# A graph layer on one Trainium2 core: attributes put into PSUM ahead of the gathering matmuls, sums by node moved to other banks

## The chip, the core and the metric

The kernel runs on one core of one Trainium2 chip. The core has a matrix engine (TensorE, PE in the profile; its weight loads stand as PEld), VectorE (DVE), ScalarE (ACT), GpSimd (POOL) and an engine that only issues transfers (SP). Matmuls write PSUM, which VectorE and ScalarE read and write; it has eight banks of 512 float32 numbers per partition. The metric is the time of one execution in microseconds (us) on the device. The kernel before took 1771.63 us, the median of 3 runs (1760.12 to 1772.58).

## What is computed

A graph of 6250 nodes and 206250 edges, 64 numbers per node and per edge, everything float32. The edges are sorted by `dst`, the node at which an edge ends.

```python
h = jnp.maximum(_layernorm(x, axis=-1), 0.0)
msg = jax.nn.relu(h[src] + edge_attr)
agg = jax.ops.segment_sum(msg, dst, num_segments=x.shape[0])
t = jax.nn.relu((h + agg) @ W1 + b1)
out = x + t @ W2 + b2
```

The large part is the middle: for each edge a row of `h` is fetched, the edge's attribute is added, and the results are summed by node.

## The kernel before

**Groups and units.** The edges are cut into 269 groups of 768: 128 partitions with 6 columns, one edge per partition and column. The rows of the first five groups are fetched by GpSimd with indirect transfers. From group 5 on, half of each group's columns (3 of 6) still come that way (`xg`), and the other 3 are fetched by TensorE; in 12 groups ("whole") all 6 columns are, as two runs of 3. Such a run of 3 columns is a unit. There are 276 units, and the main loop `for u in range(U): half(u)` (line 792) runs once for each.

**Fetching on TensorE.** All of `h` lies in SBUF, split into three bfloat16 parts that add up to the float32 value (`hp`). Fetching takes two steps, and each works on one-hot matrices that VectorE and ScalarE write ahead of time (`found`, `backs`). First, `slots_of` (line 470) collects rows of `hp` with matmuls of 32 output rows into a PSUM tile `half`, two runs of 192 numbers per tile (3 parts of 64), and `slots_out` (line 485) copies that tile on ScalarE as bfloat16 to `picked`. Two units share a set of six such tiles. Then `pick` (line 488) makes 18 matmuls of 128 by 128 by 192, six for each column, that bring each edge's three parts to its partition, in a PSUM tile `pick0` or `pick1`, by the parity of the unit.

**The four places of a column.** A pick tile holds 4 columns of 4 places of 64 numbers, two banks in all. For each of 3 columns, places 0 to 2 take the three parts. `room` (line 496), a ScalarE copy, puts the edge's attribute in place 3. VectorE then adds the four places in one reduction of 768 numbers to 192 (line 563).

**Sums by node.** `messages` (line 553) adds the DMA-fetched rows to their attributes (line 560), makes the reduction (line 563), and ScalarE writes `msg`, the relu of the group (line 565). `window_sum` (line 570) multiplies the message of a unit with a one-hot matrix of 32 nodes (`one_hot`, line 540): 12 matmul records for 6 columns. Its result, 32 numbers wide, stands in the fourth column of the pick tile of that unit's parity. `sum_into_z` (line 536) adds it to `z`, the sum of all nodes, on VectorE, two units later.

**Order.** The schedule is written out by hand. Each engine runs its queue in the order in which the code issues the work, and the framework sets the waits between engines; for PSUM it does so by bank: two engines that touch a bank are kept apart, in whatever columns. In `half(u)` the order is: loads (SP); `window_sum(u - 1)` (PE); `room(u + 1)` (ACT); twice `slots_of` and `slots_out` for the next set, and a third `slots_of`; `pick(u + 1)` (PE); `sum_into_z(u - 2)` (DVE) and, for blocks of nodes that are complete, the final layers (`blocks_behind`); `messages(u)` (DVE, then ACT); the third `slots_out` (ACT); `one_hot(u)`, and the writing of later `backs` and `found` (DVE, and on ACT `back_far`, line 455, or `back_near`, line 458). Ranks for later sets follow in small pieces.

So ScalarE's queue in a half reads: room, copy, copy, message, copy, then one of the two for `backs`. VectorE's reads: add into `z`, add of `xg`, reduction, one-hot, `backs`, `found`.

**PSUM.** The eight banks are: two pick tiles of two banks, three `half` tiles that take turns, and one tile `rows` for everything else. The attribute loads go to twelve SBUF tiles `ea` that take turns.

Of the kernel before, what the change touches and what calls it, by code (L numbers as in the profile page):

```python
# [81 lines left out]
def kernel(  # L82
# [102 lines left out]
    nc.vector.memset(z[:D, N:], 0.0)  # L185

    def attr_load(ea, g):
        if g < NG:
            nc.sync.dma_start(out=ea.rearrange("p j d -> p (j d)"),
                              in_=edge_attr[g * GE:(g + 1) * GE, :].rearrange("(p j) d -> p (j d)", j=G))  # L190
        else:
            nc.sync.dma_start(out=ea[:, G - CT:G - 1].rearrange("p j d -> p (j d)"),
                              in_=edge_attr[C * P:(C + TJ) * P, :].rearrange("(p j) d -> p (j d)", j=TJ))
            nc.sync.dma_start(out=ea[:, G - 1, :], in_=edge_attr[E - P:, :])
# [16 lines left out]
    def load(g):  # L211
        ea = edge.tile([P, G, D], F32, name="ea")
        attr_load(ea, g)
        lo, hi = first_col(g), pool_cols(g)
        if is_whole(g):
            return ea, None
        if g < F0:
            xg = lnp.tile([P, G, D], F32, name="xr", bufs=F0)
        else:
            xg = edge.tile([P, G - H, D], F32, name="xg")  # L220
        gather(xg[:, lo:], src_sb[:, g * G + lo:g * G + hi], hi - lo, x if g < RAW else h_rows)
        return ea, xg
# [99 lines left out]
    def source(c):  # L322
# [12 lines left out]
        nc.sync.dma_start(out=lines[c].rearrange("k m s -> m k s"), in_=col.rearrange("m (k s) -> m k s", k=SETS))  # L335

    def ln_head(r, n):
        xv = x_rows(r, n)
# [22 lines left out]
    def ln_turn(r, m, h):  # L361
        zv = z[:D, :NP].rearrange("d (p r) -> d p r", r=RR)
        for i in range(0, m, 4):
            n = min(4, m - i)
            pt = psum.tile([D, 4, PP], F32, name="half", bufs=3)
            for u in range(n):
# [103 lines left out]
    def slots_of(k, n0):  # L470
        ps = psum.tile([P, 2, 3 * D], F32, name="half", bufs=3)
        for u in range(2):
# [15 lines left out]
    def pick(u0, cols):  # L488
        k, i = divmod(u0, 2)
        ps = picks[u0]  # L490
        for u in cols:
            for q in range(Q):
                nc.tensor.matmul(ps[:, u, :3].rearrange("p t d -> p (t d)"), backs[k][:, q, i * H + u, :],  # L493
                                 picked[k][:, i * Q + q], start=(q == 0), stop=(q == Q - 1))

    def room(u):
        g, c0 = UNITS[u]
        picks[u] = pick_banks[u % 2]
        nc.scalar.copy(picks[u][:, :H, 3], taken[g][0][:, c0:c0 + H])  # L499

# [52 lines left out]
    def messages(u):  # L553
# [7 lines left out]
        if u >= 0:  # L561
            c0 = UNITS[u][1]
            nc.vector.tensor_reduce(ea[:, c0:c0 + H], picks.pop(u)[:, :H].rearrange("p j t d -> p j d t"), AX.X, ALU.add)  # L563
        msg = work.tile([P, G, D], F32, name="msg", bufs=3)
# [180 lines left out]
    for k in (0, 1):  # L745
        source_load(k)
        spot_load(k)
    for g in range(F0):
        enter(g + AHEAD)
        messages(g - F0)  # L750
# [67 lines left out]
    with tc.If(any_left > 0):  # L818
        nc.gpsimd.iota(wide, pattern=[[1, WB]], base=1, channel_multiplier=0, allow_small_or_imprecise_dtypes=True)
        with tc.For_i(0, NG, 1) as i:  # L820
# [3 lines left out]
            nc.vector.tensor_copy(lf, left[:, ds(i * G, G)])  # L824
            ea = edge.tile([P, G, D], F32, name="ea")
            nc.sync.dma_start(out=ea.rearrange("p j d -> p (j d)"),
# [3 lines left out]
            all_windows(combine(xa, ea, G), lf, G)  # L830
        ea = edge.tile([P, G, D], F32, name="ea")
        attr_load(ea, NG)
# [45 lines left out]
```

## Time and profile before

| | before |
|---|---|
| time, median of 3 runs | 1771.63 us (1760.12 to 1772.58) |
| time of the profiled execution | 1747.93 us |
| its span, first to last instruction | 1746.2 us |
| from `window_sum` in half(0) to the last one | 115.92 to 1737.88 us, 276 halves, 5.88 us each |
| VectorE busy, ScalarE busy | 1024.7 us (59%), 871.5 us (50%) |
| mean granted TensorE clock | 0.907 |

The profiled execution ran 1.3% below the median; 1.7 us of it lie outside of the span. The page of the profile gives busy time by engine, then the chain of work that ended last, followed back from the end, then the costliest groups of instructions with mean durations in ns and the idle time before them. "Issue" stands for time in which an engine waited for nothing that the profile shows, and "remote" for a release that it can't name. Other views show the waits in total, and the timeline: start, length, engine, line, operation, what it writes and reads, how many alike, and in brackets the idle time before it and what ended it. Matmuls are pipelined, so a busy TensorE isn't one at its peak.

### The profile page before, as it was taken

The page shows a single profiled execution, that of the slowest core. Times are in us where ns is not written, and L with a number is a line of the kernel's source. Part 1 is how long each engine was busy: PE and PEld are TensorE (multiplying, and loading weights), DVE is VectorE, ACT ScalarE, POOL GpSimd, SP SyncE. Part 2 cuts the span into 40 slices and gives each one's busy share as a digit, 9 for nine tenths or more (in the row PEclk, how much of TensorE's full clock was granted, in tenths as well). Part 3 has the DMA queues.
Part 4 walks back from the last instruction along what each step waited for, and adds up shares of the span by engine and source line. Part 5 has one row for each costly group of instructions (what it writes and reads, how often), then busy time and mean ns, then how long its engine had stood idle before and what let it go on. Part 6 is the DMA issues. An engine that isn't in the chain of part 4 may idle for free.

```text
span 1746.2 us, 54838 instructions
## 1 busy us (share of the span) xinstructions
PE 1302.7 (75%) x23181; PEld 991.3 (57%) x23181; DVE 1024.7 (59%) x2686; ACT 871.5 (50%) x1955; POOL 802.7 (46%) x798
## 2 busy tenths in 40 slices
PE   3047787778778778777777877877777877777787
PEld 2035566556557556565655655655665655565566
DVE  7346556546565665555755655654566566465576
ACT  4235455446455555554544544644554555454465
POOL 6734435444453553544544444444444445444430
PEclk9998889889897898989988988987899889898898
DMA  6223334334333442443433333333333334333341
GB/s 181 66 57 108 103 93 109 91 88 114 99 98 95 114 109 82 108 106 93 117 96 91 106 99 95 104 98 90 94 103 106 93 106 110 86 103 95 97 111 33
DMA packets 115095, 172.34 MB, mean 99 GB/s; under 512 B 28443, under 2 KB 83612, under 8 KB 114844
## 3 DMA queue, kind: packets, MB, share of 16 engines
q1 hardware_dynamic: 89752, 143.03, 27.4%
q0 software_dynamic: 25088, 25.74, 8.3%
q8 instruction: 184, 3.01, 0.7%
q14 instruction: 67, 0.55, 0.1%
q10 hardware_dynamic: 4, 0.01, 0.0%
HBM read 164.85 MB, written 3.84 MB: 97 GB/s over the span
## 4 chain that ended last, share of the span: by engine, by line
PE 64%; issue 18%; another core or an unknown queue 7%; ACT 6%; DVE 3%; POOL 1%; DMA 1%; DVEq 0%; ACTq 0%; POOLq 0%
PE pick L493 28%; PE half L478 24%; PE pick L575 8%; ACT picked L486 2%; PE rows L329 1%; ACT msg L565 1%; PE rows L592 1%; PE rows L603 1%; ACT dist L455 1%; PE rows L279 1%; POOL xg L198 1%; PE rows L277 1%; PE rows L315 0%; ACT backs L458 0%
## 5 line engine op out<-in xcount | busy, mean ns | idle before, releaser
L198 POOL DMA_INDIRECT xg<-h_rows,src_sb x754 | 768.0, 1019 | 865.4 <-DVE ea L560 688.2
L478 PE MATMUL half<-hp,found 128*32 128x192 bf16 x14352 | 500.8, 260 | 215.3 <-issue 191.8
L486 ACT CAST picked<-half 128x384 bf16<-128x384 f32 x828 | 381.1, 477 | 521.7 <-remote 321.7
L493 PE MATMUL pick<-picked,backs 128*128 128x192 bf16 x4968 | 574.6, 267 | 83.9 <-issue 64.2
L493 PEld LDWEIGHTS <-backs 128*128 128x128 bf16 x4968 | 446.6, 106 | 198.1 <-issue 179.6
L478 PEld LDWEIGHTS <-found 128*32 128x32 bf16 x14352 | 340.7, 100 | 320.7 <-issue 284.0
L538 DVE TENSOR_TENSOR z<-z,pick 128x32 f32 x281 | 53.1, 189 | 656.7 <-issue 236.4
L563 DVE TENSOR_REDUCE ea<-pick 128x192 f32<-128x768 f32 x276 | 262.5, 951 | 0.0
L465 DVE TENSOR_SCALAR backs<-spots,ids 128x768 bf16<-128x768 int16 x690 | 251.0, 415 | 0.0
L575 PE MATMUL pick<-oh,msg 128*64 128x32 f32 x3224 | 177.3, 237 | 54.6 <-ACT msg L565 29.5
L446 DVE TENSOR_SCALAR found<-sources,nodes_of 128x1536 bf16<-128x1536 int16 (+1 forms) x414 | 212.4, 542 | 0.1
L575 PEld LDWEIGHTS pick<-oh,msg 128*64 128x64 f32 x3224 | 138.4, 149 | 119.7 <-issue 53.7
L565 ACT ACTIVATE msg<-ea 128x384 f32<-128x384 f32 (+2 forms) x281 | 144.4, 514 | 24.5 <-DVE ea L563 12.8
L499 ACT COPY pick<-ea 128x192 f32<-128x192 f32 x276 | 88.6, 321 | 126.0 <-remote 69.4
L458 ACT ACTIVATE backs<-dist,ones 128x768 bf16<-128x768 bf16 x138 | 130.5, 946 | 0.3 <-ACT dist L455 0.3
L455 ACT ACTIVATE dist<-spots,far 128x768 bf16<-128x768 int16 x138 | 129.9, 941 | 0.0
L544 DVE TENSOR_TENSOR oh<-slot,slots 128x192 f32<-128x192 int16 (+2 forms) x281 | 95.7, 341 | 24.2 <-remote 24.2
L560 DVE TENSOR_TENSOR ea<-ea,xg 128x192 f32<-128x192 f32 x252 | 90.2, 358 | 3.4 <-issue 1.9
L277 PE MATMUL rows<-at,upper 128*128 128x432 f16 x46 | 17.0, 369 | 44.9 <-remote 24.1
L281 ACT CAST before<-rows 128x432 f16<-128x432 f32 x46 | 23.6, 514 | 48.4 <-remote 38.8
L332 ACT CAST source<-rows 24x64 int16<-24x64 f32 x138 | 27.6, 200 | 35.9 <-remote 27.6
L329 PE MATMUL rows<-holds,marks 128*96 128x96 f16 x276 | 27.6, 235 | 15.2 <-DVE oh L544 4.9
(102 smaller groups left out, 435.1 us busy)
## 6 DMA issues: line engine op xcount, KB each, us to landing
sources<-source_row SPq DMA_DIRECT2D x138, 384.0 KB
ea<-in_edge_attr_dram SPq DMA_DIRECT2D x268, 192.0 KB
spots<-spot_rows SPq DMA_DIRECT2D x138, 192.0 KB
xg<-h_rows,src_sb POOLq DMA_INDIRECT x754
xb<-in_x_dram SPq DMA_DIRECT2D x12, 128.0 KB
out_dram<-o SPq DMA_DIRECT2D x12, 128.0 KB
h_rows<-x SPq DMA_DIRECT2D x3, 384.0 KB
dst_sb<-in_dst_main_dram SPq DMA_DIRECT2D x1, 804.0 KB
```

Of the source, the lines that this page charges most:

```text
L198: nc.gpsimd.indirect_dma_start(out=xg[:, j, :], out_offset=None, in_=rows[:, :], in_offset=bass.IndirectOffsetOnAxis(ap=idx[:, j:j + 1], a ...
L446: nc.vector.tensor_scalar(found[k][:, b * PARTS:b * PARTS + n].rearrange("p m i s -> p (m i s)"), sources[k][:, :n * 2 * S], nodes_of[:, b ...
L455: nc.scalar.activation(dists[k], spots[k].bitcast(I16), AF.Abs, bias=far)
L458: nc.scalar.activation(backs[k][:, Q - 1].rearrange("p t s -> p (t s)"), dists.pop(k), AF.Relu, bias=ones[:, 0:1], scale=-1.0)
L465: nc.vector.tensor_scalar(backs[k][:, q].rearrange("p t s -> p (t s)"), spots[k].bitcast(I16), ids[:, q:q + 1], None, op0=ALU.is_equal)
L478: nc.tensor.matmul(ps[j * S:(j + 1) * S, u], found[k][:, m, i, :], hp[:, min(m, RR - 1)].rearrange("p t d -> p (t d)"), start=(b == 0), st ...
L486: nc.scalar.copy(picked[k][:, n0:n0 + 2], halves.pop((k, n0)))
L493: nc.tensor.matmul(ps[:, u, :3].rearrange("p t d -> p (t d)"), backs[k][:, q, i * H + u, :], picked[k][:, i * Q + q], start=(q == 0), stop ...
L544: nc.vector.tensor_tensor(oh[:, lo:hi], slot[:, g * G + lo:g * G + hi].unsqueeze(2).to_broadcast([P, n, W]), slots.unsqueeze(1).to_broadca ...
L563: nc.vector.tensor_reduce(ea[:, c0:c0 + H], picks.pop(u)[:, :H].rearrange("p j t d -> p j d t"), AX.X, ALU.add)
L565: nc.scalar.activation(msg[:, lo:hi], ea[:, lo:hi], AF.Relu)
L575: nc.tensor.matmul(pa[i * D:(i + 1) * D], msg[:, j, :], oh[:, j, :], start=(j < lo + 2), stop=(j >= hi - 2))
```

## The change

The attribute no longer has a place of its own. `room` now writes all three places of each column before the matmuls: the attribute in place 0, zeros in places 1 and 2. All 18 matmuls of `pick` accumulate onto that (none starts afresh any more), and VectorE adds three places instead of four. The zeros come from the attribute tiles, which become twice as wide: 12 fixed tiles `eas` whose second halves ScalarE fills with zeros once, before the main loop (`tails_begin`). In the usual unit the attribute and the zeros lie so that one copy of 576 numbers writes them; a unit on columns 0 to 2 of a whole group takes two copies. The result of `window_sum` moves from the pick tiles to the columns 384 to 511 of the three `half` banks, one after the other by unit; the `half` tiles become fixed banks that are handed out in turn (`next_half`). Before the main loop, four matmuls write over the whole of the pick tiles' banks with a fresh start (`banks_begin`). Each half of the main loop hands out three `half` banks, always 2, 0 and 1 in this order, and the sum of unit u stands in bank u mod 3.

```diff
+    eas = [const.tile([P, 2 * G, D], F32, name=f"ea{i}") for i in range(LOOK)]
...
     def load(g):
-        ea = edge.tile([P, G, D], F32, name="ea")
-        attr_load(ea, g)
+        ea = eas[g % LOOK]
+        attr_load(ea[:, :G], g)
...
+    half_banks = [psum.tile([P, 512], F32, name=f"half{i}", bufs=1) for i in range(3)]
+    halves_made = [0]
+
+    def next_half():
+        halves_made[0] += 1
+        return half_banks[halves_made[0] % 3]
...
     def slots_of(k, n0):
-        ps = psum.tile([P, 2, 3 * D], F32, name="half", bufs=3)
+        ps = next_half()[:, :2 * 3 * D].rearrange("p (u d) -> p u d", u=2)
...
                 nc.tensor.matmul(ps[:, u, :3].rearrange("p t d -> p (t d)"), backs[k][:, q, i * H + u, :],
-                                 picked[k][:, i * Q + q], start=(q == 0), stop=(q == Q - 1))
+                                 picked[k][:, i * Q + q], start=False, stop=(q == Q - 1), skip_group_check=True)
 
     def room(u):
         g, c0 = UNITS[u]
         picks[u] = pick_banks[u % 2]
-        nc.scalar.copy(picks[u][:, :H, 3], taken[g][0][:, c0:c0 + H])
+        parts = taken[g][0][:, H:].rearrange("p (t c) d -> p c t d", c=H)
+        if c0:
+            nc.scalar.copy(picks[u][:, :H, :3], parts)
+        else:
+            nc.scalar.copy(picks[u][:, :H, 0], taken[g][0][:, :H])
+            nc.scalar.copy(picks[u][:, :H, 1:3], parts[:, :, 1:])
...
+    def banks_begin():
+
+        for t in pick_banks:
+            flat = t.rearrange("p j t d -> p (j t d)")
+            for b in range(0, (H + 1) * 4 * D, 512):
+                nc.tensor.matmul(flat[:, b:b + 512], ones_b, mark_rows[0].rearrange("p g s j -> p (g s j)")[:, :512],
+                                 start=True, stop=True)
+
+    def tails_begin(i):
+        nc.scalar.copy(eas[i][:, G:].rearrange("p j d -> p (j d)"), zero.to_broadcast([P, G * D]))
...
-            nc.vector.tensor_reduce(ea[:, c0:c0 + H], picks.pop(u)[:, :H].rearrange("p j t d -> p j d t"), AX.X, ALU.add)
+            nc.vector.tensor_reduce(ea[:, c0:c0 + H], picks.pop(u)[:, :H, :3].rearrange("p j t d -> p j d t"), AX.X, ALU.add)
...
-        pa = pick_banks[u % 2][:, H].rearrange("p t d -> p (t d)")[:, u // 2 % AB * W:][:, :W]
+        pa = half_banks[u % 3][:, 2 * 3 * D + u // 3 % AB * W:][:, :W]
```

More of the change, by code (lines that the diff above doesn't have):

```diff
@@ L364, in ln_turn @@
             n = min(4, m - i)
-            pt = psum.tile([D, 4, PP], F32, name="half", bufs=3)
+            pt = next_half()[:D].rearrange("d (u p) -> d u p", u=4)
             for u in range(n):
@@ L747 @@
         spot_load(k)
+    banks_begin()
     for g in range(F0):
+        for i in range(g * LOOK // F0, (g + 1) * LOOK // F0):
+            tails_begin(i)
         enter(g + AHEAD)
@@ L824 @@
             nc.vector.tensor_copy(lf, left[:, ds(i * G, G)])
-            ea = edge.tile([P, G, D], F32, name="ea")
+            ea = eas[0][:, :G]
             nc.sync.dma_start(out=ea.rearrange("p j d -> p (j d)"),
@@ L830 @@
             all_windows(combine(xa, ea, G), lf, G)
-        ea = edge.tile([P, G, D], F32, name="ea")
+        ea = eas[0][:, :G]
         attr_load(ea, NG)
```

## The prediction

> **What bounds the kernel now.** I read the page first: what is busy, and what the chain that ended last is made of.
>
> ```profile
> span 1746.2 us, 54838 instructions
> ...
> PE 1302.7 (75%) x23181; PEld 991.3 (57%) x23181; DVE 1024.7 (59%) x2686; ACT 871.5 (50%) x1955; POOL 802.7 (46%) x798
> ...
> PE 64%; issue 18%; another core or an unknown queue 7%; ACT 6%; DVE 3%; POOL 1%; DMA 1%; DVEq 0%; ACTq 0%; POOLq 0%
> ```
>
> TensorE carries the chain, and 18% of it is "issue": TensorE had work and nothing to wait for, but its instructions did not come. VectorE, whose work the change shortens, holds 3%. Next the waits in total (who waited for what: us, times, longest).
>
> ```profile
> ACT picked L486 <- remote: 321.7, 147, 6.2
> PE half L478 <- issue: 191.8, 455, 1.2
> ACT picked L486 <- PE half L478: 129.4, 172, 2.7
> PE pick L493 <- issue: 64.2, 239, 0.5
> ACT pick L499 <- remote: 69.4, 43, 3.4
> ACT pick L499 <- PE pick L575: 53.6, 58, 2.9
> PE pick L575 <- ACT msg L565: 29.5, 34, 2.8
> ACT msg L565 <- DVE ea L563: 12.8, 28, 3.5
> ```
>
> TensorE's waits for instructions (191.8 and 64.2 us) are ten times its wait for messages (29.5). ScalarE waits long for the slots' matmuls (321.7 + 129.4), but hardly for VectorE: the message waited for the reduction 28 times, 12.8 us in all. So a shorter reduction by itself can give no more than that. Then one half of the main loop in the timeline, for PE, ACT and DVE.
>
> ```profile
> 909.68 0.54 PE L575 MATMUL pick<-oh,msg 128*64 128x32 f32 x12
> 910.15 1.26 PE L478 MATMUL half<-hp,found 128*32 128x192 bf16 x52
> 911.34 1.41 PE L493 MATMUL pick<-picked,backs 128*128 128x192 bf16 x15
> 913.00 0.41 PE L493 MATMUL pick<-picked,backs 128*128 128x192 bf16 x3 [0.25 <-issue]
> 913.34 0.24 PE L575 MATMUL pick<-oh,msg 128*64 128x32 f32 x1
> ```
> ```profile
> 909.96 0.94 ACT L455 ACTIVATE dist<-spots,far 128x768 bf16<-128x768 int16 x1
> 910.80 0.24 ACT L317 COPY sp<-rows 18x128 bf16<-18x128 bf16 x1
> 910.94 0.31 ACT L499 COPY pick<-ea 128x192 f32<-128x192 f32 x1
> 911.19 0.46 ACT L486 CAST picked<-half 128x384 bf16<-128x384 f32 x1
> 912.31 0.48 ACT L486 CAST picked<-half 128x384 bf16<-128x384 f32 x1 [0.66 <-PE half L478]
> 912.69 0.53 ACT L565 ACTIVATE msg<-ea 128x384 f32<-128x384 f32 x1
> ```
> ```profile
> 909.82 0.19 DVE L538 TENSOR_TENSOR z<-z,pick 128x32 f32 x1 [1.97 <-ACT msg L565]
> 910.30 0.36 DVE L560 TENSOR_TENSOR ea<-ea,xg 128x192 f32<-128x192 f32 x1 [0.30 <-issue]
> 910.58 0.95 DVE L563 TENSOR_REDUCE ea<-pick 128x192 f32<-128x768 f32 x1
> ```
>
> VectorE adds a sum into `z` at 909.82, has its reduction done at 911.53, and then the message stands in ScalarE's queue until the second slots' copy, at 912.79, is through. It ends at 913.22, and its window sum starts at 913.34. VectorE has a slack of more than a microsecond here; ScalarE's message has 0.1 us. I took this last gap, from the end of a message to the first matmul of its window sum, from the timeline for all 276 units (first and last):
>
> ```profile
> 120.20 0.53 ACT L565 ACTIVATE msg<-ea 128x384 f32<-128x384 f32 x1
> ...
> 121.28 0.51 PE L575 MATMUL pick<-oh,msg 128*64 128x32 f32 x11 [0.34 <-issue]
> ...
> 1737.41 0.42 ACT L565 ACTIVATE msg<-ea 128x256 f32<-128x256 f32 x1
> ...
> 1737.88 0.32 PE L575 MATMUL pick<-oh,msg 128*64 128x32 f32 x2 [0.78 <-ACT msg L565]
> ```
>
> It is 0.69 us in the mean; under 0.1 us in 68 units, under 0.5 in 130, under 1.0 in 205. Messages arrive nearly just in time: whatever delays them by a microsecond stops TensorE in three halves of four.
>
> **The change, part by part.** *The reduction* adds 576 numbers instead of 768.
>
> ```profile
> L563 DVE TENSOR_REDUCE ea<-pick x276: 945/951/958, 116.6 to 1734.7; 128x192 f32<-128x768 f32 x138
> L526 DVE TENSOR_REDUCE raw_v<-msg 128x6 f32<-128x384 f32 x3 | 1.7, 550 | 0.6 <-ACT msg L523 0.6
> ```
>
> The two rows (951 ns for 768, 550 for 384) give 1.04 ns a number, so 0.75 us: 0.2 us less, 276 times, 55 us of VectorE's time. The path gets it only where a message waits for VectorE, today at most the 12.8 us; below it enters the new path.
>
> *The copy ahead of the picks* grows from 192 to 576 numbers. Between 384 numbers (0.53 us, the message) and 768 (0.94, L455) 576 lie at 0.73 us, against 0.31: 0.42 more, 276 times, 116 us of ScalarE. It stands ahead of the slots' copies. Read off the timeline, ScalarE waited for matmuls before 174 of 274 first copies, which hides it; the other 100 pay up to 100 x 0.42 = 42 us. Against that the copy loses its wait for the window sum in its own bank, 53.6 us. I take zero net, bounds -54 and +42. [...]
>
> *The picks* run as they did: 15 of 18 were accumulating already. They now wait for the copy ahead, but it sits ahead of two slots' copies in ScalarE's queue, and picks come after three slots: nothing. *The start*: four matmuls and 12 copies of 384 zeros, at most 12 x 0.53 = 6.4 us of ScalarE before the loop, where it is 38.4 us busy in the first 115 us:
>
> ```profile
> 0.00:115.00 115.00, 25.72 (x235) 17.41 (x235) 59.95 (x136) 38.44 (x64) 69.61 (x80) 1.00 0.37 104
> ```
>
> (PE, PEld, DVE, ACT, POOL busy.) I take 2, bounds 0 and 6.
>
> *The sums by node* are the costly part. The framework keeps engines apart by bank. So far the add into `z` for unit u-2, at the head of VectorE's half(u), shared its bank with pick(u), which the reduction behind it needs anyway: no cost. Now it shares a `half` bank with slots that TensorE writes and ScalarE copies in that same half. As built, the add waits in half(u) for the first slots' copy (u mod 3 = 1), the second (u mod 3 = 2), or the third slots' matmuls (u mod 3 = 0). Behind the add in VectorE's queue stand the add of `xg`, the reduction, the one-hot, `backs` and `found`; for the reduction waits the message, for that the window sum at the head of TensorE's next half. Where the sum's bank is 1 (u mod 3 = 1), the window sum waits besides for the third copy, which comes behind the message: 0.43 us.
>
> From the end of a copy to the reduction's end are 0.1 (release) + 0.19 + 0.28 + 0.75 = 1.3 us; today the message starts 0.1 us before the second copy's end. So, with a little for the second release, it is late by about 1.45 us where the add waits for the second copy, 1.35 behind the third slots (16 of the 52 matmuls, 0.4 us after the second ones, whose copy would take 0.48), and 0.45 to 1.45 behind the first copy, third copy included, by how late the second was: 0.9. Less the slack of each unit, zero where that is larger, 92 units of each kind: 71 + 59 + 49 = 180 us, if TensorE stands still for all of it.
>
> [...]
>
> *What covers it* is the starved instruction supply. While TensorE waits for a message, instructions pile up behind:
>
> ```profile
> 655.03 0.69 PE L575 MATMUL pick<-oh,msg 128*64 128x32 f32 x12 [2.67 <-ACT msg L565]
> 655.65 2.28 PE L478 MATMUL half<-hp,found 128*32 128x192 bf16 x44
> 658.31 0.51 PE L478 MATMUL half<-hp,found 128*32 128x192 bf16 x6 [0.38 <-issue]
> ```
>
> After 2.67 us of standing, 56 matmuls come without a gap, then the gaps are back. If all waiting were made good so, the floor would be the new loop of waits alone, from message to message, by the distances of starts in the half shown. For u mod 3 = 1: 0.38 to the operation for `backs`, 0.84 to the copy ahead, 0.67 to the first slots' copy, 0.48 for it, 1.3, the message 0.53 and the third copy 0.43: 4.6 us. For 2, where that third copy is done: 0.84 + 0.67 + 0.38 + 0.48 + 1.3 + 0.53 = 4.2. For 0: window sum 0.47, slots 1.26, release and VectorE 1.6, message 0.53: 3.9. The mean is 4.25. Today's half takes 5.88 (from the window sum at 121.28 to that at 1737.88, by 275), but 49 are shorter than 4.25, by 41 us in all. So 41 to 180 us; the rows show relief, but gaps soon after it, so I take the middle, 110.
>
> Sum: 1747.9 + 110 + 2 = 1860 us by the profiled execution. The median of the runs lies 23.7 us above that execution; I add the 112 to the median: 1884, rounded to 1880.
>
> **The rivals.** *Hidden* (0.12): the instruction supply sets the pace, TensorE's queue makes good every wait, also in the short halves. For it speaks that 18% of the chain is issue; against it that 68 messages are just in time, hence no spare supply there. Then 1772 + 2, within 17 us.
>
> *Exposed* (0.14): nothing is made good, ScalarE's longer copy counts too: 1772 + 180 + 42 = 1994. For it: after that wait the supply failed again within a microsecond of its 56 matmuls.
>
> *Faster* (0.08): ScalarE is the one that holds the chain, by its copy ahead, which today waits for a window sum. Freed, it starts up to a window sum earlier: -53.6, with 12.8 us of waiting for the reduction, -66: 1705. It decides only if the adds into `z` find their copies done, that is, if VectorE runs over 1.3 us late already; in the half shown it is early.
>
> *The reduction is no shorter*, since it still steps over every fourth place: 0.2 us more in the new path, half of it covered as above, 28 us up, 1908; inside the forecast's range.
>
> **How the numbers follow.** 0.66 for the forecast (1813 to 1952), 0.14 exposed, 0.12 hidden, 0.08 faster; the fourth only shifts the first. The range 1768 to 1990 leaves out the faster case, about a quarter of the hidden one and half of the exposed one. One percent, 18 us, is what runs tell from no change (they spread by 12 us): faster 0.08, same 0.12, slower 0.80.
>
> **What would show it.** The add into `z` should start one to four microseconds into TensorE's half, with its idle time ended by slots' copies or slots' matmuls (L486 and L478 before); TensorE's wait for messages at the window sums should grow from 29.5 us to well over 100, and "issue" shrink by what was made good. The reduction at 0.75 us and the copy at 0.73 check the sizes. If the add starts with the half, or the message still ends as early against the second copy, the step fails; if TensorE's waits grow as told and its issue gaps shrink by as much, it is the hidden case.

## The result, and the profile after

The changed kernel took 1701.8 us (median of 6 runs, 1693.11 to 1705.29) against 1763.0 us for the kernel before (median of 6, 1737.17 to 1772.58): a ratio of 0.973, with a 95% interval of 0.966 to 0.980. (Ratios here compare fast runs alone, for the kernel before those of 1737.17 to 1760.12 us, so they are not the quotient of these medians.) It is 2.7% faster, where 1880 us had been forecast, 6% above the 1771.63 us known then. One thing must be known to read what follows: the kernel before itself took 1755 to 1765 us in some sessions on the chips and 1102 to 1105 us in others, on one chip (number 11) both. Below, the first condition is called short supply, for there TensorE shows many gaps with no release that it waits for ("issue": 256 us ahead of slots and picks before the change, where all its idle time there is 16 us in the second condition), which I read as instructions that come late, and the second full supply. This result and the profile shown before belong to short supply.

From the page of the profile after: the span, busy time by engine, and the groups that answer to those before (busy us, mean ns, then idle us ahead of them and what ended most of it).

```profile
span 1698.9 us, 54613 instructions
...
PE 1226.6 (72%) x23185; PEld 957.5 (56%) x23185; DVE 995.5 (59%) x2686; ACT 954.9 (56%) x1979; POOL 785.4 (46%) x798
...
L487 PE MATMUL half<-hp,found 128*32 128x192 bf16 x14352 | 509.6, 256 | 267.3 <-issue 243.3
L495 ACT CAST picked<-half 128x384 bf16<-128x384 f32 x828 | 365.2, 475 | 344.3 <-PE half L487 300.2
...
L502 PE MATMUL pick<-picked,backs 128*128 128x192 bf16 x4968 | 519.1, 266 | 3.5 <-ACT pick L510 2.1
...
L563 DVE TENSOR_TENSOR z<-z,half 128x32 f32 x281 | 53.0, 189 | 638.4 <-ACT picked L495 511.1
...
L588 DVE TENSOR_REDUCE ea<-pick 128x192 f32<-128x576 f32 x276 | 207.1, 750 | 0.1
L510 ACT COPY pick<-ea 128x576 f32<-128x576 f32 x264 | 168.4, 638 | 0.0
```

The reduction has the forecast length, 750 ns; the copy ahead is a little shorter than forecast, 638 ns. The add into `z` waits for slots' copies as told, 511 us in all; VectorE was idle as long ahead of it before (656.7 us in all, 638.4 after), so what is new is how late in the half that idle time ends. But the picks (L502, L493 before) had 83.9 us of idle time ahead of them, and now have 3.5. From the waits of the same kernel (us in total, times, longest):

```profile
DVE z L563 <- ACT picked L495: 511.1, 213, 4.3
...
ACT picked L495 <- PE half L487: 300.2, 206, 3.9
PE half L487 <- issue: 243.3, 560, 1.2
ACT msg L590 <- DVE ea L588: 199.1, 192, 4.6
...
PE half L600 <- ACT picked L495: 57.5, 70, 4.5
...
ACT picked L495 <- remote: 43.4, 27, 2.6
...
PE half L600 <- DVE oh L569: 20.9, 33, 0.8
PE half L600 <- ACT msg L590: 20.3, 37, 1.4
...
PE half L600 <- issue: 6.3, 18, 1.6
```

Messages wait for the reduction (199.1 us, 12.8 before), and TensorE waits at its window sums for ScalarE and VectorE, 57.5 + 20.9 + 20.3 = 99 us, where 29.5 us had been: the costs that the forecast named are there. What it did not have is on the other side: issue ahead of the picks is gone, and ScalarE's waits for slots with no named releaser fell from 321.7 to 43.4 us. Not all of that is won, for its waits put down to the slots' matmuls rose from 129.4 to 300.2 us: by the pages, all idle time ahead of the slots' copies fell from 521.7 to 344.3 us. One half in the timeline shows the new order, for PE, ACT and DVE:

```profile
580.12 0.54 PE L600 MATMUL half<-oh,msg 128*64 128x32 f32 x12 [0.70 <-DVE oh L569]
580.59 0.92 PE L487 MATMUL half<-hp,found 128*32 128x192 bf16 x35
581.94 0.27 PE L487 MATMUL half<-hp,found 128*32 128x192 bf16 x2 [0.43 <-issue]
582.68 0.29 PE L487 MATMUL half<-hp,found 128*32 128x192 bf16 x3 [0.47 <-issue]
583.42 0.45 PE L487 MATMUL half<-hp,found 128*32 128x192 bf16 x12 [0.45 <-issue]
583.79 1.66 PE L502 MATMUL pick<-picked,backs 128*128 128x192 bf16 x18
...
585.78 0.54 PE L600 MATMUL half<-oh,msg 128*64 128x32 f32 x12
```
```profile
583.52 0.86 ACT L495 CAST picked<-half 128x384 bf16<-128x384 f32 x2 [1.71 <-PE half L487]
585.15 0.52 ACT L590 ACTIVATE msg<-ea 128x384 f32<-128x384 f32 x1 [0.77 <-DVE ea L588]
```
```profile
583.96 0.19 DVE L563 TENSOR_TENSOR z<-z,half 128x32 f32 x1 [2.06 <-PE half L487]
...
584.37 0.75 DVE L588 TENSOR_REDUCE ea<-pick 128x192 f32<-128x576 f32 x1
```

TensorE stands 0.7 us, then 47 matmuls follow each other without a gap; then come three gaps, all inside the slots, and the picks run through. Of the 275 halves, 166 have three such gaps in their matmuls. In the timeline I counted the steps of 0.25 to 1.2 us from the start of one matmul to the start of the next of the same line: before 840 of them, 485 us, of which 139 us in picks, 37 in window sums and 120 between the 40th and the 58th matmul of a half; after 606, 397 us, of which none in picks or window sums and 320 in that stretch. So the gaps became fewer by 88 us, and they gathered.

The same as a table, for every kernel read below: the halves u = 0 to 274 of the main loop cut, by starts of matmuls, at their window sum, last slot, last pick and next window sum; mean us.

| kernel | supply | window sum and slots | picks | last pick to window sum | half |
|---|---|---|---|---|---|
| before | short | 2.90 | 2.33 | 0.66 | 5.89 |
| changed | short | 2.96 | 1.84 | 0.91 | 5.72 |
| moved sums alone (15) | short | 2.83 | 1.83 | 1.07 | 5.74 |
| the wait alone (17) | short | 2.92 | 1.89 | 1.36 | 6.18 |
| third copy ahead of the message (14) | short | 2.92 | 2.53 | 0.97 | 6.43 |
| seeds alone (12) | short | 2.89 | 2.54 | 0.64 | 6.07 |
| add at the end of the half (13) | short | 3.50 | 2.01 | 0.56 | 6.07 |
| before | full | 1.53 | 1.61 | 0.56 | 3.70 |
| changed (5) | full | 1.77 | 1.66 | 1.02 | 4.45 |

In the changed kernel the picks give back 0.49 us a half; standing ahead of the window sums takes 0.25, and the window sum and slots 0.06. That is 0.17 us a half, 48 us in 275 halves, as much as lies between the two profiled spans (1746.2 and 1698.9 us).

### The profile page after: what moved, and what is told of

Its sections match the earlier page's. It is cut to its first block, busy times and chain, and to the rows that moved or that the text cites. A ratio compares the mean times of both kernels' runs of the same rounds, so it can differ in the third digit from the quotient of the medians.

```text
span 1698.9 us, 54613 instructions
## 1 busy us (share of the span) xinstructions
PE 1226.6 (72%) x23185; PEld 957.5 (56%) x23185; DVE 995.5 (59%) x2686; ACT 954.9 (56%) x1979; POOL 785.4 (46%) x798
## 5 line engine op out<-in xcount | busy, mean ns | idle before, releaser
L200 POOL DMA_INDIRECT xg<-h_rows,src_sb x754 | 749.9, 995 | 827.6 <-DVE ea L585 662.4
L495 ACT CAST picked<-half 128x384 bf16<-128x384 f32 x828 | 365.2, 475 | 344.3 <-PE half L487 300.2
L487 PEld LDWEIGHTS <-found 128*32 128x32 bf16 x14352 | 325.2, 98 | 393.6 <-issue 357.1
L502 PE MATMUL pick<-picked,backs 128*128 128x192 bf16 x4968 | 519.1, 266 | 3.5 <-ACT pick L510 2.1
L502 PEld LDWEIGHTS <-backs 128*128 128x128 bf16 x4968 | 449.3, 106 | 60.5 <-issue 50.7
L563 DVE TENSOR_TENSOR z<-z,half 128x32 f32 x281 | 53.0, 189 | 638.4 <-ACT picked L495 511.1
L590 ACT ACTIVATE msg<-ea 128x384 f32<-128x384 f32 (+2 forms) x281 | 142.9, 509 | 259.2 <-DVE ea L588 199.1
L474 DVE TENSOR_SCALAR backs<-spots,ids 128x768 bf16<-128x768 int16 x690 | 279.9, 453 | 0.0
L600 PE MATMUL half<-oh,msg 128*64 128x32 f32 x3224 | 152.7, 229 | 109.5 <-ACT picked L495 57.5
L600 PEld LDWEIGHTS half<-oh,msg 128*64 128x64 f32 x3224 | 121.3, 140 | 171.8 <-ACT picked L495 75.1
L588 DVE TENSOR_REDUCE ea<-pick 128x192 f32<-128x576 f32 x276 | 207.1, 750 | 0.1
L510 ACT COPY pick<-ea 128x576 f32<-128x576 f32 x264 | 168.4, 638 | 0.0
```

What stands on the lines that cost most here:

```text
L200: nc.gpsimd.indirect_dma_start(out=xg[:, j, :], out_offset=None, in_=rows[:, :], in_offset=bass.IndirectOffsetOnAxis(ap=idx[:, j:j + 1], a ...
L474: nc.vector.tensor_scalar(backs[k][:, q].rearrange("p t s -> p (t s)"), spots[k].bitcast(I16), ids[:, q:q + 1], None, op0=ALU.is_equal)
L487: nc.tensor.matmul(ps[j * S:(j + 1) * S, u], found[k][:, m, i, :], hp[:, min(m, RR - 1)].rearrange("p t d -> p (t d)"), start=(b == 0), st ...
L495: nc.scalar.copy(picked[k][:, n0:n0 + 2], halves.pop((k, n0)))
L510: nc.scalar.copy(picks[u][:, :H, :3], parts)
L590: nc.scalar.activation(msg[:, lo:hi], ea[:, lo:hi], AF.Relu)
```

## The experiments

The first eleven fell into full supply, the others into short supply. Where no other base is named, a ratio is to the kernel before as run beside it, with its 95% interval.

**1 to 4: the parts, and the place of the add.** Their core, against the kernel before for 1 and 2, against the changed kernel for 3 and 4:

```diff
 # 1 (e1_banks); 2 (e2_sums) has it too
-        ps = psum.tile([P, 2, 3 * D], F32, name="half", bufs=3)
+        ps = next_half()[:, :2 * 3 * D].rearrange("p (u d) -> p u d", u=2)
 # 2, beside that
-        pa = pick_banks[u % 2][:, H].rearrange("p t d -> p (t d)")[:, u // 2 % AB * W:][:, :W]
+        pa = half_banks[u % 3][:, 2 * 3 * D + u // 3 % AB * W:][:, :W]
 # 3 (e3_bank2)
-        pa = half_banks[u % 3][:, 2 * 3 * D + u // 3 % AB * W:][:, :W]
+        pa = half_banks[2][:, 2 * 3 * D + u % AB * W:][:, :W]
 # 4 (e4_zlate)
-        sum_into_z(u - LAG)
-        blocks_behind(u - LAG)
         messages(u)
+        sum_into_z(u - LAG)
+        blocks_behind(u - LAG)
```

> The kernel before, with only the three half banks made fixed and handed out in turn (the same banks in the same order); sums by node stay in the pick tiles, the attribute keeps its place, four parts are added. It takes away 527 waits of TensorE on its own earlier matmuls, at the first matmul of a slots' group, and no other wait. Theory A (these waits slow TensorE's queue, and their end is the gain of 61 us): about 1700 us, ratio 0.965 to 0.98, and the late releases of slots' groups to ScalarE (321.7 us before) go. Theory B (the gain is that the copy ahead no longer waits for a window sum in its bank) and theory C (the gain is the seeding with a reduction of three parts): no change, 0.995 to 1.005, 1755 to 1770 us.

> The first experiment, and the sums by node moved to the half banks as in the changed kernel; the attribute keeps its place, the copy ahead is 192 numbers, the reduction 768. The copy ahead waits for no window sum any more (274 waits go), 222 signals of picks go, and the add into z gets its wait for slots' copies or matmuls. Theory A: no lower than the first experiment, 1700 us or up to 40 above it by the new wait of the add. Theory B: 1690 to 1715 us, ratio about 0.97 where the first experiment stands at 1.00. Theory C: above the kernel before, 1780 to 1860, for it has the new wait without the seeds.

> The changed kernel with all sums by node in one half bank, the one of the first slots' group; so the add into z waits for the first slots' copy in every half, instead of the first, the second or the third slots in turn, and no window sum waits for a third copy. If the add's new wait is paid for (my prediction's terms of 71, 59 and 49 us for the three kinds, of which some is covered): 20 to 60 us below the changed kernel, 1640 to 1680. If it is covered by the starved instruction supply: as the changed kernel, 1695 to 1710.

> The changed kernel with the add into z (and the final layers behind it) issued behind messages(u) instead of ahead of it: the reduction no longer stands behind the add's wait for slots. The third slots' copy on ScalarE now waits for the add in some halves. If the add's wait is paid for: 40 to 110 us below the changed kernel, 1590 to 1660. If the instruction supply covers it: 1690 to 1710, with TensorE's waits for messages gone and its issue gaps longer by as much.

| | us | ratio |
|---|---|---|
| 1, fixed banks | 1105.2 | 1.003 (1.000 to 1.005) |
| 2, fixed banks and moved sums | 1329.4 | 1.205 (1.200 to 1.210) |
| 3, changed, one bank for all sums | 1285.6 | 1.165 (1.160 to 1.171) |
| 4, changed, add behind the reduction | 1135.1 | 1.030 (1.025 to 1.034) |

All four expectations were built on a kernel before of 1763 us, and it took 1103.2. Within this condition they say this: without TensorE's waits on its own matmuls the time is the same (1105.2 us); moving the sums costs 226 us by itself; waiting for the first copy only helps a little (1285.6); and with the reduction ahead of the add most of the loss is gone (1135.1). That is the forecast's mechanism, paid in full. It left the measured gain unexplained.

**5 and 6: the changed kernel again, and the add later still.** The fifth is the changed kernel as it is. The sixth, against it:

```diff
-        sum_into_z(u - LAG)
-        blocks_behind(u - LAG)
         messages(u)
...
         one_hot(u)
+        sum_into_z(u - LAG)
+        blocks_behind(u - LAG)
```

> The changed kernel itself, once more, beside the kernel before. In the first four experiments the kernel before took 1103 us, not 1763, and TensorE's slots and picks came almost without gaps. Theory S (the two results belong to two conditions: where TensorE is starved of instructions the add's new wait is covered, where it is not the wait is paid for): if the kernel before takes about 1103 us again, the changed kernel takes 1290 to 1330 (the second experiment's 1329, less up to 30 by the shorter reduction, not below the third's 1286), ratio 1.17 to 1.20; if it takes about 1760 us, ratio 0.97 again. Theory T (the changed kernel is the faster one everywhere): ratio 0.97 also where the kernel before takes 1103 us, so 1070.

> The changed kernel with the add into z (and the final layers behind it) issued behind the third slots' copy and the one-hot, that is still later than in the fourth experiment: no copy on ScalarE waits for the add there, but the next half's slots do where they share its bank. If the fourth experiment's 1135 us were still above the kernel before by its add standing ahead of the one-hot: 1080 to 1105 us where the kernel before takes 1103 us. If the next half's slots now wait for VectorE: 1135 to 1200. Where the kernel before takes about 1760 us: 1690 to 1720.

The changed kernel took 1310.3 us, ratio 1.186 (1.181 to 1.192): theory S held, the sign of the change depends on the condition. The sixth took 1171.6, 1.062 (1.057 to 1.066): later than behind the reduction is worse again. By the waits, the next half's slots wait somewhat longer for VectorE's `found` than in the fourth (40.8 us, 21.9 there) and the window sums for slots' copies (32.6 us, 7.7 there); the slots' waits for the add itself, which had been expected, come to 4.8 us.

**The kernel before in full supply, and 7: seeds alone.** The kernel before was run once more for its profile. The seventh is the changed kernel with the old place of the sums. Its result leaves attributes out (its window sums start afresh in a bank that holds seeds; the twelfth, whose window sums accumulate there, has them all); it does the same work in the same order, so its time is read here:

```diff
-        pa = half_banks[u % 3][:, 2 * 3 * D + u // 3 % AB * W:][:, :W]
+        pa = pick_banks[u % 2][:, H].rearrange("p t d -> p (t d)")[:, u // 2 % AB * W:][:, :W]
```

> The kernel before itself, once more, for a profile of the condition in which the experiments ran. If it takes about 1104 us: TensorE's issue gaps at slots and picks (191.8 and 64.2 us in the profile shown) nearly gone, ScalarE's waits with no named releaser for slots (321.7 us) gone, operations of VectorE and ScalarE with the same durations as before (reduction 0.95 us, message 0.51). If it takes about 1760 us: the profile shown before, within 2%.

> The changed kernel with its sums by node back in the fourth column of the pick tiles: so only the seeding is left, with the copy ahead of 576 numbers that waits for a window sum again, and the reduction of three parts; the fixed half banks stay. If a window sum's fresh start reached beyond its own columns, the third column's attributes would be left out of the result. Where the kernel before takes 1104 us: theory S puts all of the loss on the add's wait, so 1085 to 1130 (0.2 us less per reduction against 0.32 us more per copy); if the longer copy is a cost of its own that the path pays, up to 1190. Where the kernel before takes about 1760 us: 1690 to 1715 if the gain came with the shorter reduction or the lost self-waits, 1750 to 1790 if it came with the moved sums.

The kernel before took 1105.9 us. Its page, and its waits:

```profile
span 1104.2 us, 54838 instructions
...
PE 1004.1 (91%) x23181; PEld 869.2 (79%) x23181; DVE 1013.9 (92%) x2686; ACT 866.2 (78%) x1955; POOL 813.5 (74%) x798
...
L493 PE MATMUL pick<-picked,backs 128*128 128x192 bf16 x4968 | 462.8, 248 | 2.2 <-ACT pick L499 1.3
...
L478 PE MATMUL half<-hp,found 128*32 128x192 bf16 x14352 | 356.9, 249 | 13.9 <-ACT dist L455 6.5
```
```profile
ACT picked L486 <- PE half L478: 51.3, 216, 1.1
...
ACT msg L565 <- DVE ea L563: 35.6, 66, 3.7
...
PE pick L575 <- ACT msg L565: 24.0, 23, 2.8
```

The program is the same, and VectorE and ScalarE are busy for as long as before (1013.9 and 866.2 us; 1024.7 and 871.5 in short supply). TensorE's gaps are nearly gone (24 of the steps counted above, 14 us), and so are ScalarE's waits without a named releaser. The seeds alone took 1099.1 us, 0.996 (0.993 to 0.999): the shorter reduction and the longer copy together are worth four microseconds. The loss is all from the moved sums. In the changed kernel of the fifth run:

```profile
ACT msg L590 <- DVE ea L588: 261.3, 252, 4.7
DVE z L563 <- ACT picked L495: 250.9, 185, 3.4
...
PE half L600 <- ACT picked L495: 87.4, 85, 4.6
...
PE half L600 <- ACT msg L590: 37.9, 73, 1.2
```
```profile
434.35 0.54 PE L600 MATMUL half<-oh,msg 128*64 128x32 f32 x12 [0.44 <-ACT msg L590]
434.83 1.26 PE L487 MATMUL half<-hp,found 128*32 128x192 bf16 x52
436.10 1.65 PE L502 MATMUL pick<-picked,backs 128*128 128x192 bf16 x18
...
438.72 0.54 PE L600 MATMUL half<-oh,msg 128*64 128x32 f32 x12 [0.59 <-ACT msg L590]
```
```profile
435.97 0.86 ACT L495 CAST picked<-half 128x384 bf16<-128x384 f32 x2
438.15 0.52 ACT L590 ACTIVATE msg<-ea 128x384 f32<-128x384 f32 x1 [1.32 <-DVE ea L588]
```
```profile
436.95 0.19 DVE L563 TENSOR_TENSOR z<-z,half 128x32 f32 x1 [0.82 <-ACT picked L495]
...
437.36 0.75 DVE L588 TENSOR_REDUCE ea<-pick 128x192 f32<-128x576 f32 x1
```

The second copy ends at 436.83, the add follows, and the message starts 1.32 us after that copy, with TensorE standing at the end. From window sum to window sum are 4.37 us.

**8 to 11: TensorE's half made longer by work.** Each pair is the kernel before and the changed one with the same edit:

```diff
 # 8 and 9 (p1_before_long, p2_after_long), ahead of the loop in slots_of
+        for m in range(4):
+            nc.tensor.matmul(ps.rearrange("p u d -> p (u d)"), ident_b, hp[:, 2 * m:2 * m + 2].rearrange("p r t d -> p (r t d)"),
+                             start=True, stop=True)
 # 10 and 11 (p3_before_thrice, p4_after_thrice)
-            for b in range(sets):
+            for b in list(range(sets)) * 3:
```

> The kernel before, with four more matmuls of 128 by 128 by 384 ahead of every group of slots, written over by the group's own: TensorE's half becomes longer by work (12 matmuls of about 0.17 us, 2.0 us), not by a lack of instructions. Where the kernel before takes 1104 us: 1104 + 276 x 2.0 = 1650 us, in all theories. It is the yardstick for the next one.

> The changed kernel with the same additional matmuls. Theory L (what covers the add's wait is only that TensorE's half is longer than the loop from a slots' copy by way of the add, the reduction and the message to the next window sum, some 4.4 us): within 1% of the kernel before with the same matmuls, the 206 us are gone. Theory E (only a queue short of instructions, that fills while TensorE stands, covers it): TensorE loses at each message what it lost without the extra work, so 150 to 220 us above the one before. Theory F (the rival of my prediction: the changed kernel is the faster one, by 2 to 3%, wherever TensorE's half is long, for its copy ahead waits for no window sum): 1600 to 1620.

> The kernel before with each slots' group computed three times over: 104 more matmuls and weight loads of 20 ns per half, so more instructions at TensorE's full rate, three times as many in the slots. If the supply of instructions holds on this chip: 1104 + 276 x 2.1 = 1680 us, without issue gaps. If it does not, issue gaps of 0.6 us appear as in the profile of the kernel before, and the time is over 1750.

> The changed kernel with each slots' group computed three times over. Theory L: within 1% of the kernel before with the same work, if no issue gaps appear. If they do, and the gain of 2.7% belongs to a starved queue: 2 to 4% below it. Theory E without gaps: 150 to 220 us above it.

They took 1758.3 and 1793.5 us (ranges 1757.3 to 1758.8 and 1792.0 to 1799.0), 1844.0 and 1883.4. The changed kernel is 35 us (2.0%) and 39 us (2.1%) the slower one. So with halves as long as in short supply (6.1 us in the eighth, for its matmuls took 2.4 us and not 2.0) some 170 of the 206 us are covered by length alone, a little less than theory L said (within 1%), and theories E and F fall. But no length of half turned the sign. The thrice computed slots did show gaps (121.7 us of issue in 142 of them, from the waits), single ones of 0.86 us in the mean; that did not turn it either.

**12 and 13: in short supply, seeds alone, and the changed kernel without the wait.** The twelfth is the seventh with window sums that accumulate too, so that seeds and sums can share a bank:

```diff
 # 12 (e8_seeds), against the seventh
+        at = u // 2 % AB
+        if at % 2 == 0:
+            nc.scalar.copy(picks[u][:, H].rearrange("p t d -> p (t d)")[:, at * W:(at + 2) * W],
+                           zero.to_broadcast([P, 2 * W]))
...
-            nc.tensor.matmul(pa[i * D:(i + 1) * D], msg[:, j, :], oh[:, j, :], start=(j < lo + 2), stop=(j >= hi - 2))
+            nc.tensor.matmul(pa[i * D:(i + 1) * D], msg[:, j, :], oh[:, j, :], start=False, stop=(j >= hi - 2), skip_group_check=True)
 # 13 (e9_zend), against the changed kernel: from ahead of messages(u) to behind back and find
+        sum_into_z(u - LAG)
+        blocks_behind(u - LAG)
         chunk(u + 14, rank_at)
```

> The seeding without the moved sums: sums by node stay in the pick tiles' fourth column, window sums accumulate too, onto zeros that a ScalarE copy of 64 numbers writes every other time that a bank comes round. So the add into z has its old, early wait, the reduction is 0.75 us, the copy ahead 0.64 us and behind a window sum. Where the kernel before takes 1104 us: as the seventh experiment's 1099, 1090 to 1106. Where it takes about 1760 us: 1690 to 1715 if the gain there came with the seeds or the lost self-waits, 1745 to 1780 if with the moved sums.

> The changed kernel with the add into z (and the final layers behind it) at the end of VectorE's half, behind the writing of backs and found: nothing of VectorE's own stands behind its wait for slots' copies, but the next half's slots wait for the add where they share its bank. Where the kernel before takes 1104 us: 1170 to 1260, above the 1135 and 1172 of the two earlier places, if it is now TensorE that waits for VectorE; 1105 to 1130 if not. Where it takes about 1760 us: 1750 to 1790 if TensorE's standing at the window sums is what made the gain, 1690 to 1715 if it is not.

Beside a kernel before of 1765.4 us they took 1785.9, 1.012 (1.006 to 1.018), and 1801.4, 1.024 (1.018 to 1.030). So in short supply neither the seeds nor the lost self-waits (both kernels have lost them) make a gain; and with the add moved away from the head of VectorE's half the gain is gone. The add still waits for the slots' copies there, only at the end of VectorE's half:

```profile
DVE z L563 <- ACT picked L495: 499.6, 204, 4.5
```

**14 to 16: standing by another means, the moved sums alone, the changed kernel again.** The fourteenth, against the kernel before (the other two are experiments 2 and 5 as they were):

```diff
-        messages(u)
         if now:
             for n0 in later:
                 slots_out(k + 1, n0)
+        messages(u)
```

> The kernel before with one exchange in ScalarE's queue: the third slots' copy ahead of the message, not behind it. The message, and with it the window sum at the head of TensorE's next half, comes 0.5 to 1 us later; the sums stay in the pick tiles, nothing is seeded. Theory P (where TensorE is short of instructions, standing at the window sums makes its later gaps fewer than it costs): where the kernel before takes about 1765 us, 1 to 3% below it, 1715 to 1750, with the gaps gathered at one place of the half. Theory N (standing is only lost or at best made good): 1765 to 1850. Where the kernel before takes 1104 us, in both: 1150 to 1260.

> The second experiment again (fixed half banks and moved sums, no seeds, reduction of 768 numbers). Where the kernel before takes about 1765 us: theory P 1700 to 1750, for the add waits as in the changed kernel and the message comes 0.2 us later still; theory N 1765 to 1880. Where the kernel before takes 1104 us: 1329 again.

> The changed kernel again. Where the kernel before takes about 1765 us: 1700 to 1725, ratio 0.96 to 0.98, if the first result holds for that condition; about 1770 or more if it was of that one session. Where the kernel before takes 1104 us: 1310 again.

The kernel before took 1761.0 us here; the three 1897.3, 1.079 (1.070 to 1.088); 1701.6, 0.966 (0.958 to 0.974); and 1705.0, 0.969 (0.961 to 0.977). The gain comes again, and the moved sums make all of it without any seed. Theory P falls: standing at the window sums by itself does not help (1897.3 us lies above the range of theory N too). In the fourteenth TensorE stands for messages, and its gaps (873 steps, 505 us) and ScalarE's late releases do not go:

```profile
ACT picked L486 <- remote: 533.9, 238, 3.4
...
PE pick L575 <- ACT msg L565: 106.8, 125, 2.6
```

**17: the wait alone.** Against the kernel before:

```diff
+    seen = const.tile([P, 1], BF16, name="seen")
...
+        if now:
+            nc.vector.tensor_copy(seen, picked[k + 1][:, first[u % 3 != 1], :1])
         sum_into_z(u - LAG)
```

> The kernel before with one small VectorE copy of one number per partition, from the first (u mod 3 = 1) or second slots' copy of the half, ahead of the add into z: VectorE's add, reduction and one-hot wait for that copy as in the changed kernel, but the sums by node stay in the pick tiles, and the copy ahead still waits for its window sum. Where the kernel before takes about 1765 us: theory W (VectorE's wait for the slots' copy ahead of the reduction makes the gain) 1700 to 1730; theory R (the copy ahead, freed of the window sum, has a part in it) 1740 to 1850. Where the kernel before takes 1104 us, in both: 1290 to 1350, which would show that the wait alone carries the loss of 206 to 226 us there.

It took 1831.2 us beside 1754.9, 1.047 (1.041 to 1.053). Theory W falls as it was put; the time lies in the range of theory R, which by itself does not show that the copy ahead has the part that R gives it. From its waits:

```profile
DVE seen L662 <- ACT picked L487: 614.5, 260, 4.3
...
PE half L479 <- issue: 211.5, 566, 0.9
...
PE pick L576 <- ACT msg L566: 102.8, 112, 4.5
PE pick L576 <- DVE backs L466: 77.8, 46, 4.9
```

But it does half of what the moved sums do: issue ahead of picks is gone, the steps counted above fell to 389 us, 307 of them between the 40th and the 58th matmul (378 and 301 in the fifteenth), and the picks take 1.89 us as in the fifteenth (1.83). What differs is the standing: 1.36 us ahead of a window sum, against 1.07 there and 0.91 in the changed kernel. In the fifteenth the copy ahead does not wait for a window sum, and ScalarE is not idle ahead of it at all; here it is idle 53.0 us there. TensorE's window sums wait 77.8 us for VectorE's `backs` here, 24.0 in the fifteenth. This run has a small copy more on VectorE, and waits for the second copy also where the changed kernel waits for the third slots. How much of the 0.3 us belongs to which was not taken apart.

## Why the prediction was wrong, point by point

- **The reduction, the picks.** 0.75 us as forecast; it had no part in the path (seeds alone: 0.996 in full, 1.012 in short supply, with ScalarE's added zeros).
- **The copy ahead.** 0.64 us instead of 0.73, my estimate between the rows of two other operations (0.53 us for 384 numbers, 0.94 for 768). Its price on the path was put at zero, and the seeds alone bear that out. That it no longer waits for a window sum I priced within -54 to +42; of that only the difference between 15 and 17 speaks, and not by itself.
- **The start.** Two microseconds more were forecast, within 0 to 6; the window sum at the head of half(0) begins at 116.44 us instead of 115.92, 0.5 us later, by one profile each.
- **The sums by node: the delay.** Right in kind, a little too large. That the waits go by bank, in whatever columns, stands in the rows: before, the copy ahead waited 58 times, 53.6 us, for a window sum in other columns of its bank; now the add into `z` waits 511.1 us for slots' copies, which read other columns than it does. By the timeline over 267 halves in full supply a message starts 0.30 us after the end of the second copy in the kernel before, and 1.16 us after it in the changed one, 0.86 us more; I had 0.9 to 1.45. The second copy itself ends 0.5 us later there (2.06 and 2.56 us after the window sum's start). In full supply the changed kernel is 206 us slower and the moved sums alone 226, near the 180 (222 with the copies) that the prediction gave for the wait with nothing covering it.
- **The sums by node: what covers it.** This step failed. "So 41 to 180 us; the rows show relief, but gaps soon after it, so I take the middle, 110." That instructions pile up behind a TensorE that stands was my reading; the rows show 56 matmuls without a gap after 2.67 us of standing, and no run shows instructions that wait in a queue. I let the shortage only make good some of the standing. The profiles show more: the second copy no longer ends 4.48 us after the window sum's start but 3.71 (means over 267 halves), so the delay behind it moves a message by just 0.14 us. TensorE's gaps fell by 88 us, and by the table the stretch from a window sum to the last pick became 0.42 us shorter, 116 us in all, while its standing rose by 0.25, 68 us in all. So in place of a cost of 41 to 180 us, the two profiles show a gain of 48, and the moved sums alone (15) make it. The lower bound of 41 excluded a gain without a reason for it.
- **The rival on the other side.** "Faster" came out at 1705, within 4 us, by luck and not as it was put: it was to decide "only if the adds into `z` find their copies done", and they wait 511 us for them; and the 12.8 us of messages waiting for the reduction, which it counted as won, became 199.1. What the runs show instead is a pattern. Where an operation of VectorE waits for the slots' copies in each half, most of the gaps lie between the 40th and the 58th matmul: 320 of 397 us in the changed kernel, 301 of 378 in 15, 307 of 389 in 17, and 302 of 459 in 13, where the add waits at the end of VectorE's half. In the kernels without that wait they do not: 120 of 485 us before, 123 of 444 in 12, 205 of 505 in 14. But gathered gaps alone are no gain: 13 loses in its slots (3.50 us to the last slot), 17 by standing (1.36 us). To keep the standing short takes something that 17 lacks and 15 has, of which the freed copy ahead is the nearest; that is argued, not shown.
- **The signs.** "Issue" was to shrink by what was made good: from 279.4 to about 250 us, while the waits at window sums grew by 69. By that the prediction would have read a loss of some 40 us, since it had no sign for ScalarE's waits ahead of the slots' copies (521.7 to 344.3 us in all), which is where their chain became shorter: the second copy starts 1.18 us after the start of its last matmul, where it was 2.02.

What is shown: the sign differs between the two conditions (ratios of 0.973 and 0.969 in short supply, 1.186 in full); the loss in full supply is the add's wait (1310.3 us, and 1135.1 with the add behind the reduction); the gain in short supply is of the moved sums alone (0.966), and goes with fewer gaps, gathered in the slots. Open is why gaps gather and become fewer where VectorE waits for the slots' copies, and what makes the conditions differ; that it is the supply of instructions was not shown.

None of the versions tried beats both kernels in both conditions; in full supply the seeds alone gain 0.4% (with attributes left out), and lose 1.2% in short supply (with all of them, and ScalarE's added zeros).

## What to carry to other kernels

Ask first of a profile whether its bound belongs to the program or to the session: of the chain, "issue" was 18% in one condition and 3% in the other, and the same edit is 2.7% faster in the first and 18.6% slower in the second. The wait behind a shared bank was priced well by its loop (copy, add, reduction, message, window sum) where TensorE shows few gaps: 180 us, 222 with the copies, for 206 and 226 measured. Where its half is made of gaps, 41 to 180 us of loss were forecast and a gain of 48 came: there the price had no lower bound, for nothing excluded a gain. And to find what a change of several parts does, run the parts in the condition in which it was measured: here moved sums alone, seeds alone and the wait alone came to -3.4%, +1.2% and +4.7%.

## What the runs showed of the hardware

- The same program took 1103 and 1763 us, a factor of 1.6. From the pages of the kernel before, the queue of instruction transfers (number, MB, share of 16 engines' span), in short and in full supply:

```profile
q8 instruction: 184, 3.01, 0.7%
```
```profile
q8 instruction: 184, 3.01, 1.1%
```

0.7% of 16 engines' 1746 us and 1.1% of their 1104 us are both about 195 us, 1.06 us for each transfer of 16 KB. So these did not become slower, and TensorE's gaps came all the same.
- In short supply a slots' copy on ScalarE starts long after the start of the last matmul of its group. For the first copy of a half that is 1.40 us in the kernel before and 1.78 in the changed one, for the second 2.02 and 1.18; in the kernel before in full supply 0.34 and 0.39 (means over 267 halves each).
- The granted clock was 0.907 and 0.914 in the two profiles of the result, 0.85 to 0.93 in all of short supply, and 0.96 to 0.99 in full supply. From the windows of the kernel before in short supply (start and end, length, busy us and matmuls on PE, then PEld, DVE, ACT, POOL, and the granted clock ahead of the DMA share):

```profile
692.80:696.20 3.40, 0.74 (x16) 0.53 (x16) 3.00 (x8) 1.60 (x3) 1.93 (x2) 1.00 0.06 10
696.20:703.00 6.80, 5.46 (x64) 3.88 (x65) 3.96 (x12) 1.21 (x5) 4.69 (x5) 0.50 0.60 170
703.00:706.40 3.40, 2.36 (x68) 1.69 (x65) 2.87 (x8) 2.08 (x5) 1.75 (x2) 0.99 0.07 15
```

In the first 3.40 us TensorE has 16 matmuls (0.74 us busy) at a granted clock of 1.00; in the 6.80 us behind them the granted clock is 0.50, and then 0.99. The 18 picks that lie mostly in the stretch at 0.50 take 2.93 us, against 1.66 in the half of the changed kernel shown above. What lowered the clock there, this one stretch does not show:

```profile
700.49 2.93 PE L493 MATMUL pick<-picked,backs 128*128 128x192 bf16 x18 [0.35 <-issue]
```
